# Reordering the front and the end of the first attention in a fused two-attention kernel

## The chip, the cores and the metric

The kernel runs on one core of one Trainium2 chip, as one program. The time is device microseconds; the median of three runs before the change is 1600.74 us, the lowest 1598.55 and the highest 1603.12. A profile is one execution recorded by the hardware profiler; its span runs from the first to the last instruction.

## The reference, cut to what matters

The program computes four residual blocks on 1024 tokens of width 512, all in float32. Only the first block and the entry of the second are touched by the change.

```python
x = x + attn_a(layernorm(x), wq, bq, wk, bk, wv, bv, wo, bo)   # 32 query heads of 16, 8 key groups, softmax over 1024 keys
x = x + ffn(layernorm(x))                                      # dense layer plus top-2 of 8 low-rank experts
x = x + attn_b(layernorm(x), ...)                              # 32 query heads of 128, 8 key groups, causal, 4-bit weights
x = x + ffn(layernorm(x))
```

The first attention's output keeps an unusual order: `out` is swapped to (head, dimension, token) and then reshaped to rows of 512, before `wo`.

## The kernel before, in words

**Engines and order.** TensorE's instructions run in the order in which the code writes them (`tc.manual_schedule` with TensorE alone, L505). The order on VectorE (DVE), ScalarE (ACT), GpSimd (POOL) and the DMA queues of SyncE (SP) and POOL is chosen by the builder's scheduler, which may draw an instruction ahead of others written before it; every queue then runs in its order. So the norm that is written after the pair loop (L549 to L557) has its statistics and rows on DVE and ACT inside the loop in the trace of before, at 407 to 424 us, while its transposes on TensorE stand after the loop.

**Tiling of the first attention** (`attention_a`, L202). 32 heads in 16 pairs of two heads. For a pair, `qs` holds both heads' queries and `ks` the group's keys, each stacked as high and low parts in 64 partitions, and this twice: partitions 0 to 63 (`low`) and 64 to 127 (`high`) hold the same, so that two matmuls on different halves of the array can run beside each other. The stacks are filled by SBUF-to-SBUF DMAs of 64 KB (16 partitions of 4 KB): `stack_keys` (L291) issues 8 for a group of two pairs, `stack_queries` (L297) 16 for a pair. There are three buffers of each (`NS = 3`), so three pairs' queries are stacked in the front.

**Scores for the maximum.** `half_score(i, rows)` (L332) is one matmul of 128 queries against 512 keys into one of three PSUM buffers `sc` (L339) and a maximum over it on DVE (L348). 32 of these make a pair; after the last, three small DVE operations leave the pair's maxima in `largest`. `place_largest` (L358) transposes them on TensorE (L362), copies them on ACT (L364) and sends two DMAs on SP into `ms_q` (L366), from where a second matmul subtracts them in `exponentials` (L375): a score matmul of the transposed kind (L380), the maxima's matmul (L388), and the exponential on ACT (L392). `weighted` (L406) multiplies the exponentials by the values.

**The front.** `keys`, `queries` (L288, through `split`, L269) are projections of four chunks of the contraction; a chunk is two matmul instructions. Between the chunks of `queries(1, 1)` to `queries(3, 1)` the function `lead` (L500) issues scores, so that scores run ahead of the loop: 20 calls of two scores, 40 in all; after the score with number 34 it calls `place_largest` for the first pair.

**The pair loop** (L517 on). For each pair and each of eight blocks of keys (`kt`) one step: `side_by_side` alternates a `low` chain (four scores and one exponential) with a `high` chain (three exponentials); then `place_largest` where maxima are due, and `weighted` of the step before. At `kt` 3 the `tail` (L427) of the pair before is normalised and transposed back into `o_sbs`. At `kt` 5 and 7 of pairs 4, 8 and 12 `project_out(a, h)` (L447) multiplies four pairs' output by `wo` (eight matmul instructions, L453) and adds the product to `x_sb` (L460). At `kt` 7 the stacks three pairs on are refilled, and at pair 12 the expert weights of the second block are loaded into `shared`, whose room the queries of pairs 8 to 15 had.

**The end of the stage.** After the loop: the norm of token blocks 0 to 2 (`stats` L154, `scale` L159 to L161 with a square root on ACT, `rows` L167 and L175, `turned` L190 with eight transposes a block), the last pair's `tail`, and `project_out(3, 0)` and `(3, 1)` between the blocks' transposes. Then the expert part begins with `hidden` (L579), and the norm of block 3.

Of the kernel before, what the change touches and what calls it, by code (L numbers as in the profile page):

```python
# [11 lines left out]
F32 = mybir.dt.float32  # L12
# [29 lines left out]
def kernel(  # L42
# [77 lines left out]
    def place_ffn_weights(room):  # L120
        at = 0
        for name, n, width in ("base", NC_, C), ("ar", NC_, AR), ("b", 1, C), ("bias", 1, C):
            fw[name] = room[:, at : at + n * width].rearrange("p (c o) -> p c o", o=width)
            at += n * width
        return room[:, :at]

    def load_ffn_weights():
        nc.sync.dma_start(fw["ar"][:, :, : E * R], w_a.rearrange("(c p) o -> p c o", p=P))
        nc.sync.dma_start(fw["ar"][:, :, E * R :], w_router.rearrange("(c p) o -> p c o", p=P))
        nc.sync.dma_start(fw["base"], w_base.rearrange("(c p) o -> p c o", p=P))  # L130
        nc.sync.dma_start(fw["b"][:, 0, :], w_b)
        nc.gpsimd.dma_start(fw["bias"][:, 0, :], b_base.partition_broadcast(P))
# [69 lines left out]
    def attention_a():  # L202
# [6 lines left out]
        with ExitStack() as ph:  # L209
# [78 lines left out]
            def queries(c, half, *between):  # L288
                split(q_hls[c], ts(half, C), lambda k: wq_n[:, c, k], bq_sb[:, c : c + 1], *between)

            def stack_keys(g, *engs):  # L291
                for r in range(8):
                    engs[r % len(engs)].dma_start(
                        ks[g % NS][ts(r, DA)].bitcast(F32), k_hl[ts(g, DA), r % 4 // 2].bitcast(F32)
                    )

            def stack_queries(pair, *engs):  # L297

                q, g = qs[pair % NS], pair // 2
                for h in range(2):  # L300
                    row = 2 * (2 * (pair % 2) + h) + g % 2
                    for r in range(8):
                        engs[r % len(engs)].dma_start(
                            q[ts(r, DA), h].bitcast(F32),
                            q_hls[g // 2][ts(row, DA), r % 2].bitcast(F32),
                        )
# [51 lines left out]
            def place_largest():  # L358
                for pair in list(large):
                    both = large.pop(pair)  # L360
                    mp = st_ps.tile([P, C], F32, tag="st", name="mp")
                    nc.tensor.transpose(mp[:, :P], both.bitcast(F32), ident)  # L362
                    mT = work.tile([32, P], F32R, tag="mT", name="mT")
                    nc.scalar.copy(mT, mp[:32, :P])  # L364
                    for r in (0, 64):
                        nc.sync.dma_start(  # L366
                            ms_q[pair % 2][r : r + 2]
                            .bitcast(F32)
                            .rearrange("h j (t q) -> h (j t) q", q=P),
                            mT.bitcast(F32),  # L370
                        )
# [3 lines left out]
            def exponentials(pair, kt, u, rows):  # L375

                if u == 0:
                    pTs[pair, kt] = work.tile([P, 4, C], F32, tag="pT", name="pT", bufs=3)
                st = st_ps.tile([P, C], F32, tag="st", name="st")
                nc.tensor.matmul(  # L380
                    st,
                    ks[pair // 2 % NS][rows, ts(kt, P)],
                    qs[pair % NS][rows, u // 2, ts(u % 2, C)],
                    start=True,
                    stop=False,
                )
                yield
                nc.tensor.matmul(  # L388
                    st, ones[rows], ms_q[pair % 2][rows, u // 2, ts(u % 2, C)], start=False, stop=True
                )  # L390
                yield
                nc.scalar.activation(pTs[pair, kt][:, u], st, AF.Exp, scale=DA**-0.5)  # L392

            def chain(*parts):
                for part in parts:
                    yield from part

            def side_by_side(*two):

                two = list(two)  # L400
                while two:
                    for one in list(two):
                        if next(one, two) is two:
                            two.remove(one)
# [39 lines left out]
                        ALU.mult,  # L444
                    )

            def project_out(a, h):  # L447

                py = st_ps.tile([P, C], F32, tag="st", name="py")
                for c in range(NC_):
                    nc.tensor.matmul(  # L453
                        py,
                        o_sbs[a][:, 4 * h + c, :],
                        wo_n[:, c, :],
                        start=(c == 0),
                        stop=(c == NC_ - 1),
                    )
                nc.vector.tensor_tensor(x_sb[:, a, h, :], x_sb[:, a, h, :], py, ALU.add)  # L460

            def keys(half):
# [5 lines left out]
            stack_queries(0, nc.sync, nc.gpsimd)  # L468
            keys(1)
            stack_keys(0, nc.sync)  # L470
            stack_keys(1, nc.gpsimd)
            stack_queries(1, nc.sync)
            stack_queries(2, nc.sync)

            bo_b = wk_n.rearrange("p k o -> p (k o)").rearrange("p (i o) -> p i o", i=1)
# [11 lines left out]
            def next_score(rows):  # L487
                nonlocal n_score
                n_score += 1
                if n_score <= 32 * PAIRS:  # L490
                    yield from half_score(n_score - 1, rows)

            def scores(n):
                for _ in range(n // 2):
                    side_by_side(next_score(low), next_score(high))


            ahead = iter((2,) * 20)

            def lead():  # L500
                scores(next(ahead))
                if n_score == 34:
                    place_largest()

            with tc.manual_schedule(engines={mybir.EngineType.PE}):  # L505
                for t in range(NT):
                    values(t)
                queries(1, 0)
                queries(1, 1, lead)
                for c in (2, 3):  # L510
                    for half in range(2):
                        queries(c, half, lead)

                wo_n = wq_n.rearrange("p c k o -> p c (k o)")
                nc.sync.dma_start(wo_n, wo.rearrange("(c p) o -> p c o", p=P))
                behind = None
                for pair in range(PAIRS):  # L517
                    for kt in range(NT):
                        side_by_side(
                            chain(  # L520
                                next_score(low),
                                next_score(low),
                                next_score(low),
                                exponentials(pair, kt, 2, low),
                                next_score(low),
                            ),
                            chain(*[exponentials(pair, kt, u, high) for u in (0, 1, 3)]),
                        )
                        if kt % 2 == 0:
                            place_largest()  # L530
                        if behind is not None:
                            weighted(*behind)
                        behind = pair, kt
                        if kt == 3:
                            for item in tails:
                                tail(*item)
                            tails.clear()
                        if kt in (5, 7) and pair % 4 == 0 and pair:
                            project_out(pair // 4 - 1, (kt - 5) // 2)
                        if kt == 7 and pair + NS < PAIRS:  # L540
                            if (pair + NS) % 2 == 0:
                                stack_keys((pair + NS) // 2, nc.sync)
                            stack_queries(pair + NS, nc.sync)
                            if pair + NS == PAIRS - 1:
                                place_ffn_weights(shared)
                                load_ffn_weights()
                weighted(*behind)

                for a in range(3):  # L549
                    norm.stats(a)  # L550
                norm.scale(0, 3)
                for item in tails:
                    tail(*item)
                for a in range(3):
                    xn = wq_in[:, 2 * (a % 2) : 2 * (a % 2) + 2]
                    norm.rows(a, xn)
                    norm.turned(a, xn, bank, False, to_xT)  # L557
                    if a:
                        project_out(3, a - 1)


    class Experts:
# [607 lines left out]
```

## Time and profile before

| what | us |
|---|---|
| median of three runs | 1600.74 |
| the profiled execution | 1601.31 |
| its span | 1599.5 |
| PE busy (matmul row) | 1531.5 (96%) |
| DVE busy | 1241.1 (78%) |
| ACT busy | 783.0 (49%) |
| POOL busy | 482.6 (30%) |
| first projection (keys) starts | 16.7 |
| first score starts | 45.96 |
| pair loop runs | about 84 to 488 |
| hidden layer of the experts starts | 499.6 |

The mean granted clock of TensorE is 0.987 of full speed. Read the busy share of PE with care: matmuls are pipelined and their ends are modelled, so a busy PE is not a PE at its peak; the granted clock stands beside it in the rows by stretch. An idle stretch in the timeline is written behind the instruction that ends it, as "[idle before <-what released it]". The idle time of an engine that is not the bound costs nothing, so waits are looked up at the place of the change and not in the sums over the program.

### The profile page before, as it was taken

The numbers are of one execution on the slowest core, as the hardware profiler recorded it, in microseconds if no ns is written. First come the engines' busy times: TensorE is split into PE (matmuls) and PEld (weight loads), VectorE is DVE, ScalarE is ACT, GpSimd is POOL, SyncE is SP. The second block draws the span as 40 slices with busy tenths as digits, with TensorE's granted clock in tenths as the row PEclk, the third lists the DMA queues.
The fourth block names the chain that finished last, engine by engine and source line by source line (L and its number), as shares of the span: only waits on it lengthen the run. The fifth ranks groups of instructions, "written<-read, shape, count | busy, mean of one in ns | idle before, by whom it ended". The sixth has DMA issues, their size and how long they took to land.

```text
span 1599.5 us, 24080 instructions
## 1 busy us (share of the span) xinstructions
PE 1531.5 (96%) x8119; PEld 990.9 (62%) x8119; DVE 1241.1 (78%) x2290; ACT 783.0 (49%) x1694; POOL 482.6 (30%) x382
## 2 busy tenths in 40 slices
PE   7899999999999989999999999999999999999978
PEld 4244444444445457777777777777777777777764
DVE  4689888799755686788888878888788788788763
ACT  2067666576673245544544544444444444454420
POOL 5200000000103154436336336335435335333120
PEclk9899999999999989999999999999999999999999
DMA  5432322324304133333334334333333334333311
GB/s 126 81 81 47 54 49 48 66 36 88 91 3 110 66 105 125 108 139 124 116 131 139 112 119 135 116 119 126 120 120 121 109 120 129 105 112 129 140 50 53
DMA packets 98010, 158.63 MB, mean 99 GB/s; under 512 B 14320, under 2 KB 53936, under 8 KB 97504
## 3 DMA queue, kind: packets, MB, share of 16 engines
q1 hardware_dynamic: 97024, 155.46, 32.6%
q0 software_dynamic: 864, 1.64, 0.7%
q8 instruction: 65, 1.06, 0.3%
q14 instruction: 57, 0.47, 0.1%
HBM read 33.03 MB, written 6.05 MB: 24 GB/s over the span
## 4 chain that ended last, share of the span: by engine, by line
PE 80%; DVE 12%; ACT 3%; issue 2%; DMA 2%; SPq 1%; POOL 0%; ACTq 0%; DVEq 0%; POOLq 0%
PE pc L888 16%; PE sc L846 15%; PE po L413 7%; PE sc L339 6%; PE pp L782 5%; DVE m L348 5%; PE pp L783 5%; PE tp L878 5%; PE py L782 3%; PE py L783 3%; PE bank L591 3%; PE pp L273 2%; PE st L380 2%; PE py L453 2%; PE st L388 2%
## 5 line engine op out<-in xcount | busy, mean ns | idle before, releaser
L348 DVE TENSOR_REDUCE m<-sc 128x1 f32<-128x512 f32 x512 | 320.7, 681 | 37.3 <-PE st L380 21.7
L855 ACT ACTIVATE x_sb<-sc,m 128x768 f32<-128x768 f32 (+7 forms) x256 | 189.7, 741 | 317.1 <-DVE m L851 311.2
L392 ACT ACTIVATE pT<-st 128x512 f32<-128x512 f32 x512 | 264.7, 603 | 125.6 <-PE st L388 111.7
L846 PE MATMUL sc<-kT,qT 128*128 128x512 f32 (+3 forms) x768 | 293.1, 491 | 4.5 <-ACT x_sb L855 2.9
L851 DVE TENSOR_REDUCE m<-sc 128x1 f32<-128x768 f32 (+7 forms) x256 | 192.7, 753 | 132.5 <-PE sc L849 130.9
L888 PE MATMUL pc<-xT,v_sb 128*128 128x256 f32 (+1 forms) x1024 | 248.5, 373 | 5.0 <-DVE acc L796 2.5
L339 PE MATMUL sc<-ks,qs 64*128 64x512 f32 x512 | 187.0, 455 | 9.8 <-DMA ks<-k_hl 4.5
L857 DVE TENSOR_SCALAR x_sb<-x_sb,total 128x768 f32<-128x768 f32 (+7 forms) x256 | 190.0, 743 | 4.6 <-DVE total L856 0.3
L888 PEld LDWEIGHTS pc<-xT,v_sb 128*128 128x128 f32 x1024 | 176.0, 190 | 21.8 <-DVE acc L796 3.2
L846 PEld LDWEIGHTS sc<-kT,qT 128*128 128x128 f32 x768 | 139.6, 193 | 74.8 <-issue 63.8
L339 PEld LDWEIGHTS sc<-ks,qs 64*128 64x128 f32 x512 | 83.5, 186 | 158.5 <-DVE m L348 128.1
L380 PE MATMUL st<-qs,ks 64*128 64x512 f32 x512 | 177.4, 425 | 2.9 <-ACT pT L392 1.7
L388 PE MATMUL st<-ms_q,ones 64*128 64x512 f32 x512 | 179.0, 414 | 0.3 <-DMA ms_q<-mT 0.3
L923 DVE SCALAR_TENSOR_TENSOR shared<-py,o_sc,shared 128x512 f32<-128x512 f32 x248 | 176.1, 739 | 3.8 <-PE py L783 3.7
L808 POOL TENSOR_TENSOR qT<-acc,cos_sb 128x512 f32<-128x512 f32 x62 | 81.7, 1318 | 298.6 <-DVE total L856 203.1
L782 PE MATMUL pp<-x_hl,w 128*128 128x512 f32 x384 | 167.4, 436 | 1.9 <-DVE acc L796 1.3
L879 ACT COPY xT<-tp 128x512 f32<-128x512 f32 (+2 forms) x320 | 137.2, 471 | 63.9 <-PE tp L878 63.6
L783 PE MATMUL pp<-x_hl,w 128*128 128x512 f32 x384 | 152.7, 398 | 2.4 <-DVE x_hl L740 2.4
L690 POOL TENSOR_SCALAR w<-r 128x512 fp32r<-128x512 int32 x80 | 123.5, 1544 | 102.9 <-PE pp L783 69.8
L796 DVE SCALAR_TENSOR_TENSOR acc<-pp,q_sc,acc 128x512 f32<-128x512 f32 x192 | 142.9, 745 | 13.4 <-ACT acc L794 7.0
L878 PEld LDWEIGHTS tp<-ident_r,moved 128*128 128x128 f32 x1152 | 125.3, 141 | 37.0 <-issue 2.2
L413 PE MATMUL po<-pT,v_sb 128*32 128x512 f32 x1024 | 137.5, 608 | 0.0
(169 smaller groups left out, 2176.4 us busy)
## 6 DMA issues: line engine op xcount, KB each, us to landing
turned<-acc SPq DMA_DIRECT2D x160, 128.0 KB
moved<-x_sb SPq DMA_DIRECT2D x32, 512.0 KB
moved<-x_sb SPq DMA_DIRECT2D x32, 448.0 KB
moved<-x_sb SPq DMA_DIRECT2D x32, 384.0 KB
moved<-x_sb SPq DMA_DIRECT2D x32, 320.0 KB
qs<-shared SPq DMA_DIRECT2D x128, 64.0 KB
r<-in_qwq_dram SPq DMA_DIRECT2D x32, 256.0 KB
r<-in_qwo_dram SPq DMA_DIRECT2D x32, 256.0 KB
```

The costliest lines, as they stand in the source:

```text
L339: nc.tensor.matmul(sc, qs[pair % NS][rows, jj, ts(t, P)], ks[pair // 2 % NS][rows, ts(half, C)], start=True, stop=True,)
L348: nc.vector.tensor_reduce(ms[pair][:, at : at + 1], sc, AX.X, ALU.max, negate=True)
L380: nc.tensor.matmul(st, ks[pair // 2 % NS][rows, ts(kt, P)], qs[pair % NS][rows, u // 2, ts(u % 2, C)], start=True, stop=False,)
L388: nc.tensor.matmul(st, ones[rows], ms_q[pair % 2][rows, u // 2, ts(u % 2, C)], start=False, stop=True)
L392: nc.scalar.activation(pTs[pair, kt][:, u], st, AF.Exp, scale=DA**-0.5)
L413: nc.tensor.matmul(po[ts(u, 32), :], v_sb[:, kt, pair // 2, :], pT[:, u], start=(kt == 0), stop=(kt == NT - 1),)
L782: nc.tensor.matmul(ps, lhsT, high, start=True, stop=False)
L783: nc.tensor.matmul(ps, lhsT, low, start=False, stop=True)
L846: nc.tensor.matmul(sc[:, k0:k1], qT[:, ts(t, P)], kT[:, k0:k1], start=True, stop=(k1 < keys))
L851: nc.vector.tensor_reduce(m, sc[:, :keys], AX.X, ALU.max, negate=True)
L878: nc.tensor.transpose(tp[:, k - k0, :].bitcast(F32R), p[:, ts(k, P)], ident_r)
L888: nc.tensor.matmul(pc[:, 2 * P * i + lo : 2 * P * (i + 1)], v_sb[:, k, ts(g, DB)], place[pair][:, k, lo:], start=(k == 0), stop=(k == 2 * ...
```

## The change

All of it is in `attention_a`. In the front, all 16 DMAs of the two groups' key stacks are issued on SP, the second group's behind the queries of pair 1; before, the second group's eight were on POOL. `lead` issues three, three and no scores in turn, five times, and two at the end: 32 scores over the 16 chunks of `queries(1, 1)` to `queries(3, 0)`. In `queries(3, 1)` only the second chunk is followed by something: `place_largest` for the first pair and three scores. So 35 scores lead instead of 40, and the pair loop takes a fifth score, at the end of the `high` chain, as long as the lead is short, which it is at five steps.

At the end, `project_out(2, 1)` moves from pair 12 to behind the loop, with the last `tail` between its second and third chunk; `project_out(3, *)` stand ahead of the transposes of the norm; the third block's `xn` has a buffer of its own; and the expert weights are placed and loaded at pair 15, `kt` 1, instead of pair 12, `kt` 7.

```diff
@@ -444,7 +444,7 @@
                         ALU.mult,
                     )
 
-            def project_out(a, h):
+            def project_out(a, h, between=lambda: None):
 
 
 
@@ -457,6 +457,8 @@
                         start=(c == 0),
                         stop=(c == NC_ - 1),
                     )
+                    if c == 1:
+                        between()
                 nc.vector.tensor_tensor(x_sb[:, a, h, :], x_sb[:, a, h, :], py, ALU.add)
 
             def keys(half):
@@ -468,8 +470,8 @@
             stack_queries(0, nc.sync, nc.gpsimd)
             keys(1)
             stack_keys(0, nc.sync)
-            stack_keys(1, nc.gpsimd)
             stack_queries(1, nc.sync)
+            stack_keys(1, nc.sync)
             stack_queries(2, nc.sync)
 
             bo_b = wk_n.rearrange("p k o -> p (k o)").rearrange("p (i o) -> p i o", i=1)
@@ -491,25 +493,36 @@
                     yield from half_score(n_score - 1, rows)
 
             def scores(n):
-                for _ in range(n // 2):
-                    side_by_side(next_score(low), next_score(high))
-
-
-            ahead = iter((2,) * 20)
-
-            def lead():
-                scores(next(ahead))
-                if n_score == 34:
-                    place_largest()
+                end = min(n_score + n, 32 * PAIRS)
+                while n_score < end:
+                    if n_score % 2 == 0 and n_score + 1 < end:
+                        side_by_side(next_score(low), next_score(high))
+                    else:
+                        side_by_side(next_score(high if n_score % 2 else low))
 
             with tc.manual_schedule(engines={mybir.EngineType.PE}):
                 for t in range(NT):
                     values(t)
                 queries(1, 0)
+
+
+                ahead = iter((3, 3, 0) * 5 + (2,))
+
+                def lead():
+                    scores(next(ahead))
+
                 queries(1, 1, lead)
-                for c in (2, 3):
-                    for half in range(2):
-                        queries(c, half, lead)
+                for half in range(2):
+                    queries(2, half, lead)
+                queries(3, 0, lead)
+
+                def first_pair():
+                    if n_score == 32:
+                        place_largest()
+                        scores(3)
+
+                ahead = iter((0, 1, 0, 0))
+                queries(3, 1, lambda: next(ahead) and first_pair())
 
                 wo_n = wq_n.rearrange("p c k o -> p c (k o)")
                 nc.sync.dma_start(wo_n, wo.rearrange("(c p) o -> p c o", p=P))
@@ -524,7 +537,10 @@
                                 exponentials(pair, kt, 2, low),
                                 next_score(low),
                             ),
-                            chain(*[exponentials(pair, kt, u, high) for u in (0, 1, 3)]),
+                            chain(
+                                *[exponentials(pair, kt, u, high) for u in (0, 1, 3)],
+                                *[next_score(high)] * (n_score < 32 * pair + 4 * kt + 40),
+                            ),
                         )
                         if kt % 2 == 0:
                             place_largest()
@@ -535,28 +551,31 @@
                             for item in tails:
                                 tail(*item)
                             tails.clear()
-                        if kt in (5, 7) and pair % 4 == 0 and pair:
+                        if kt in (5, 7) and pair in (4, 8, 12) and (pair, kt) != (12, 7):
                             project_out(pair // 4 - 1, (kt - 5) // 2)
                         if kt == 7 and pair + NS < PAIRS:
                             if (pair + NS) % 2 == 0:
                                 stack_keys((pair + NS) // 2, nc.sync)
                             stack_queries(pair + NS, nc.sync)
-                            if pair + NS == PAIRS - 1:
-                                place_ffn_weights(shared)
-                                load_ffn_weights()
+                        if kt == 1 and pair == PAIRS - 1:
+                            place_ffn_weights(shared)
+                            load_ffn_weights()
                 weighted(*behind)
+                project_out(2, 1, lambda: tail(*tails.pop()))
 
                 for a in range(3):
                     norm.stats(a)
                 norm.scale(0, 3)
-                for item in tails:
-                    tail(*item)
+                project_out(3, 0)
+                project_out(3, 1)
                 for a in range(3):
-                    xn = wq_in[:, 2 * (a % 2) : 2 * (a % 2) + 2]
+                    xn = (
+                        wq_in[:, 2 * a : 2 * a + 2]
+                        if a < 2
+                        else q_hls[0][:, 0].bitcast(F32).rearrange("p (i o) -> p i o", i=2)
+                    )
                     norm.rows(a, xn)
                     norm.turned(a, xn, bank, False, to_xT)
-                    if a:
-                        project_out(3, a - 1)
 
 
     class Experts:
```

## The prediction

> **What bounds the kernel now.** I read the page's chain first, then stretches of the front, then the timeline there, then the same for the end of the first attention.
>
> ```profile
> PE 80%; DVE 12%; ACT 3%; issue 2%; DMA 2%; SPq 1%; POOL 0%; ACTq 0%; DVEq 0%; POOLq 0%
> ```
>
> The chain ends on TensorE almost everywhere, so a microsecond of TensorE idleness inside a stage, or of TensorE work at half clock, is paid in full. In the rows by stretch the columns are: stretch, its length, busy us of PE, PEld, DVE, ACT and POOL with their instructions, granted clock, share of the DMA engines, GB/s.
>
> ```profile
> 28.00:46.00 18.00, 14.09 (x82) 9.95 (x80) 4.42 (x11) 1.37 (x2) 8.69 (x18) 0.98 0.83 132
> 46.00:66.00 20.00, 19.37 (x44) 6.44 (x44) 14.65 (x24) 1.37 (x2) 8.83 (x4) 0.84 0.61 104
> ...
> 42.00:46.00 4.00, 0.09 (x2) 0.07 (x1) 0.70 (x1) 0.00 (x0) 0.43 (x1) 0.93 0.82 200
> 46.00:50.00 4.00, 3.37 (x4) 0.99 (x4) 1.38 (x2) 0.00 (x0) 4.00 (x2) 0.50 0.57 101
> ...
> 74.00:78.00 4.00, 1.91 (x5) 0.61 (x5) 2.26 (x7) 0.25 (x1) 0.00 (x0) 0.77 0.01 4
> 78.00:82.00 4.00, 4.00 (x8) 1.14 (x7) 1.29 (x2) 0.00 (x0) 0.00 (x0) 0.50 0.03 8
> ```
>
> See two holes in TensorE (42 to 46, and 74 to 76) and after each a half-rate clock. The timeline names what they wait for:
>
> ```profile
> 38.35 6.54 SPq L293 DMA_DIRECT2D ks<-k_hl  x8
> 44.94 20.23 SPq L303 DMA_DIRECT2D qs<-q_hl  x32
> 45.96 0.76 PE L339 MATMUL sc<-ks,qs 64*128 64x512 f32 x1 [3.91 <-DMA ks<-k_hl]
> 47.35 0.76 PE L339 MATMUL sc<-ks,qs 64*128 64x512 f32 x1 [0.63 <-DMA ks<-k_hl]
> 59.16 1.29 DVE L348 TENSOR_REDUCE m<-sc 128x1 f32<-128x512 f32 x2 [0.28 <-PE sc L339]
> 76.40 0.45 PE L362 MATMUL mp<-ident,largest 128*128 128x128 f32 x1 [2.09 <-DVE largest L353]
> ```
>
> First hole: the stack of the first keys. Second: the pair's maxima, which VectorE has not finished. Between them a lead (2 scores) and a chunk of projection recur every 1.48 us, or 6.1 us per four with the projection's own VectorE step (54.02 to 60.12); VectorE is busy 8 x 0.62 + 0.74 = 5.7 of these.
>
> At the end of the stage:
>
> ```profile
> 410.42 3.70 PE L453 MATMUL py<-wq_n,o_sb 128*128 128x512 f32 x8
> 417.21 1.28 ACT L392 ACT_TABLE_LOAD   x1
> 419.16 0.50 PE L380 MATMUL st<-qs,ks 64*128 64x512 f32 x1 [1.73 <-ACT pT L392]
> 415.90:421.60 5.70, 3.97 (x25) 1.43 (x23) 5.63 (x14) 4.68 (x9) 0.59 (x1) 0.94 0.59 137
> ...
> 488.61 0.66 PE L433 MATMUL pt<-ident,oT 128*128 128x128 f32 x4 [0.78 <-DVE oT L422]
> 495.18 3.60 PE L453 MATMUL py<-wq_n,o_sb 128*128 128x512 f32 x8
> 499.60 5.80 PE L579 MATMUL bank<-shared,xT 128*128 128x136 f32 x48 [0.83 <-issue]
> ```
>
> A usual step of the pair loop takes 2.71 us (weighted at 89.53, 92.23, 94.94). The step with `project_out(2, 1)` takes 6.5. The next two take 5.65 and 3.87: the first norm's statistics, square root, table load and rows, written behind the loop, were drawn forward into it, and the exponentials stand behind them on ACT.
>
> **1. Order of the stacks.** Eight DMAs leave POOL (8 x 0.485 us of issue) and stand on SP between the queries of pairs 1 and 2. Nothing of the first keys' stack is moved on SP; what goes is the 0.5 MB that competed with it, for the engines were 0.8 to 0.9 busy from 30 to 46. Before, SP's issues were stretched until 39.65 (the seventh query DMA held it 3.38 us). Free of this, I let the first key DMA issue between 37.2 and 38.4, then one per 0.6 us, plus the 2.9 us from the eighth's issue (44.31) to the score it released: high keys at 44.3 to 45.4 instead of 47.35. Projections run out at 42.05 as before, so a hole of 2.3 to 3.3 us stays. **The rule against the row:** the Trainium skill's page "TensorE: Matmul & The Clock Gate", Part 1, has the clock halved only after an idle window of some 3.4 us; by it this hole might cost no clock and the gain would be about 5. The trace shows 2.09 us idle at 74.30 followed by clock 0.50, and both drops (45.4 and 76.2, from the mean clocks) lie nine times 3.41 us apart: what counts is how empty a window is, and 42.0 to 45.4 stays empty. So I take the half clock as kept and a gain of **2.0** (bounds 1.5 and 5).
>
> What it costs SP: the page "DMA: Bandwidth & Descriptors", "Issuing engines are not separate DMA queues", says that several issuing engines save only sequencer time, usually small beside the transfer; moving eight DMAs would then be free. The rows differ: 132 GB/s with two queues, 104 with SP alone at engine share 0.61, so SP's issue (20.23 / 32 = 0.63 us) is the limit, and the move adds 8 x 0.63 = 5 us of SP. SP would end near 43 + 40 x 0.63 = 68. Behind it stands the DMA of the maxima, not due before 71: hidden, by 3 us. The bo load and POOL's four additions come forward; nobody waits for them.
>
> **2. Threes.** Six scores per three projection chunks, as before, so the work is equal. VectorE needs 6 x 0.62 + 0.74 x 3/4 = 4.27 us per three chunks against 6.1 x 3/4 = 4.58 now. The added wait is the third score's, for the third of three buffers; behind it on PE stands a chunk, covered by VectorE's backlog in the empty third slot. Leads 4 to 16 are 13 chunks: 13/3 x 0.31 = **1.3** (0.5 to 2).
>
> **3. Last projection and maxima.** Before, from the sixteenth lead (72.34) to the loop's first score (84.0) were 11.6 us: four chunks, eight scores, the 2.09 us wait, half clock to 83. After: two chunks (1.7 us) follow the sixteenth lead, the maxima are ready some 2.9 us after it (two reductions, the projection's step, three of 0.2), so a wait of 1.0; transpose 0.3, three scores 0.5, two chunks 1.7: 5.6 us. The first exponential then needs the maxima's DMA: 0.86 us from transpose to issue, 2.95 from issue to landing (462.19 to 465.14, where TensorE last waited for it), 3.8 in all against 3.0 of cover: 0.8 more. Gain 11.6 - 6.4 = **5.2** (2.5 if this wait empties a clock window).
>
> **4. Five steps of five scores.** VectorE has 4 x 0.62 = 2.48 of 2.71 us; five make 3.1, and the fifth buffer wait stays below that. 5 x 0.4 = **2.0 lost** (1 to 3).
>
> **5. `project_out(2, 1)` out of the loop.** 3.65 us leave pair 12. With the residual missing, the norm can't be drawn forward: 5.65 + 3.87 - 2 x 2.71 = 4.1 leave the next steps, with two table loads. Gain **7.75** (7 to 7.75).
>
> **6. The new end.** Before, 487.8 to 499.6: 11.8 us. After, from 487.8: two chunks of (2, 1) 1.7 (they cover the 0.78 wait for `oT`), tail 0.6, two chunks 1.7, `project_out(3, *)` 6.9, 24 transposes 2.6: 13.6, then the evacuation of the last bank 0.8: 14.4, **2.6 lost** (2 to 4). The norm chain starts when (2, 1) ends at +4.1: addition 0.7, statistics 0.9, root 0.3, two small steps 0.5, rows 0.8, with gaps +8; the transposes want it at +11. The cover is `project_out(3, *)`; without it some 4 us would stand open. The third `xn` frees a wait that was hidden anyway.
>
> **7. Expert weights' loads.** SP and POOL issue them later: base 395.59, the rest at 418 to 420, first read at 499.6. Even issued near 467 they have 30 us. SP has one pair of maxima to move there (462.19). Zero.
>
> Sum: -2.0 - 1.3 - 5.2 + 2.0 - 7.75 + 2.6 = -11.65. The profiled execution took 1601.3 (span 1599.5 and 1.8 around it), so 1589.7; the median shown is 0.6 lower: **1589.1**, chance 0.50.
>
> **Rivals.**
> - Half clock at the maxima (0.20): the waits of step 3 fall in one window. For it: 2.09 us sufficed. Against: the forecast's 1.0 and 0.8 lie 3 us apart. +2.7: 1591.8.
> - No half clock after the first hole (0.13): keys in time, or windows lie differently. -3: 1586.
> - Something drawn forward elsewhere (0.10): engines other than TensorE are ordered by the builder, and the norm's later place may block ACT or VectorE in the expert part, as it did at 416; half of the 7.75 is given back, and two further microseconds: 1595 to 1598, at worst 1606.
> - **Slower: SP becomes the bound (0.07).** The maxima's DMA waits behind 40 stacking DMAs. At 0.71 us each it is late; at about 0.99 the whole gain is gone; at the 1.29 of 27.92 to 38.23 (8 in 10.31 us) the loop starts 22 us late: 1611. Against: 0.63 over 32 in a row with POOL's queue empty.
>
> **Range.** Best ends of all terms: 5 + 2 + 6 - 1 + 7.75 - 2 = 17.75, 1583; worst: 1.5 + 0.5 + 2.5 - 3 + 7 - 4 = 4.5, 1596; the fourth case stretches it to 1598. Within 0.3% (4.8 us, what a measurement here can't tell from none) means above 1595.9. Faster: 0.50 + 0.20 + 0.13 + 0.02 = 0.85; same: 0.06 of the fourth and 0.02 of SP's case, 0.08; slower 0.07.
>
> **What would show it.** First high score near 45 and not 47.35; one half-clock stretch before the loop, not two; the loop's first score near 75; five steps near 3.1 us; no long step after pair 12; hidden layer beginning 14.4 us after the last weighted sum. Wrong if the maxima's DMA issues after 75, if a table load splits the pair loop, or if the transposes at the end wait for VectorE.

## The result, and the profile after

The median is 1592.69 us over eleven runs (1589.33 to 1599.53), against 1600.06 us over eleven of the kernel before (1595.37 to 1605.39). The ratio is 0.9958, with a 95% interval of 0.994 to 0.9976: a gain of 6.7 us, at least 3.8 and at most 9.6. It is about 60% of the 11.65 that the sum promised. The profiled execution took 1591.28 us, span 1589.2, mean granted clock 0.992.

The chain that ended last, by engine, has hardly changed:

```profile
PE 81%; DVE 12%; ACT 3%; issue 2%; DMA 1%; SPq 1%; ACTq 0%; DVEq 0%
```

The front by stretch, with the columns that the prediction names:

```profile
42.00:46.00 4.00, 1.14 (x3) 0.18 (x1) 1.44 (x2) 0.54 (x1) 4.00 (x3) 1.00 0.91 110
46.00:50.00 4.00, 3.00 (x6) 1.09 (x7) 1.29 (x2) 0.00 (x0) 3.72 (x2) 0.61 0.64 108
50.00:54.00 4.00, 4.00 (x7) 1.40 (x7) 1.89 (x3) 0.00 (x0) 0.00 (x0) 0.53 0.66 106
...
74.00:78.00 4.00, 3.29 (x11) 1.47 (x10) 2.96 (x7) 0.58 (x2) 0.00 (x0) 1.00 0.00 0
78.00:82.00 4.00, 3.75 (x16) 1.46 (x14) 3.31 (x7) 2.40 (x3) 0.00 (x0) 1.00 0.27 78
```

The hole at 42 to 46 and the half clock behind it are still there. The second pair, the hole at the maxima and half clock to 83, is gone: the clock is 1.00 from 74 to 82. The timeline says which wait is where:

```profile
32.00 0.75 DVE L276 SCALAR_TENSOR_TENSOR k_hl<-pp,bk_sb,k_hl 128x512 fp32r<-128x512 f32 x1 [2.68 <-ACT k_hl L275]
38.42 5.41 SPq L293 DMA_DIRECT2D ks<-k_hl  x8
44.23 0.47 PE L339 MATMUL sc<-ks,qs 64*128 64x512 f32 x1 [1.55 <-DMA ks<-k_hl]
47.00 0.80 PE L339 MATMUL sc<-ks,qs 64*128 64x512 f32 x2 [2.30 <-DMA ks<-k_hl]
...
59.00 0.73 PE L339 MATMUL sc<-ks,qs 64*128 64x512 f32 x3
59.66 1.12 PE L273 MATMUL pp<-xT,wq_n 128*128 128x512 f32 x2
60.72 1.25 PE L339 MATMUL sc<-ks,qs 64*128 64x512 f32 x3
61.90 1.98 PE L273 MATMUL pp<-xT,wq_n 128*128 128x512 f32 x4
64.34 3.68 DVE L348 TENSOR_REDUCE m<-sc 128x1 f32<-128x512 f32 x6 [0.47 <-PE sc L339]
...
76.66 0.30 PE L362 MATMUL mp<-ident,largest 128*128 128x128 f32 x1 [0.71 <-DVE largest L353]
77.36 1.43 SPq L366 DMA_DIRECT2D ms_q<-mT  x2
80.42 0.50 PE L388 MATMUL st<-ms_q,ones 64*128 64x512 f32 x1 [0.23 <-DMA ms_q<-mT]
...
406.86 1.07 PE L413 MATMUL po<-pT,v_sb 128*32 128x512 f32 x8
408.87 0.49 PE L388 MATMUL st<-ms_q,ones 64*128 64x512 f32 x1 [0.28 <-DMA ms_q<-mT]
410.22 1.06 PE L413 MATMUL po<-pT,v_sb 128*32 128x512 f32 x8
...
475.77 2.40 PE L413 MATMUL po<-pT,v_sb 128*32 128x512 f32 x16
477.09 1.28 ACT L159 ACT_TABLE_LOAD   x1
478.10 1.98 PE L453 MATMUL py<-wq_n,o_sb 128*128 128x512 f32 x4
480.36 8.75 PE L453 MATMUL py<-wq_n,o_sb 128*128 128x512 f32 x20
488.95 1.91 PE L190 MATMUL tp<-ident,wq_in 128*128 128x128 f32 x16
492.58 1.63 PE L598 MATMUL bank<-shared,xT 128*128 128x136 f32 x12 [0.83 <-ACT rstd L159]
```

Read it from the top: TensorE waits 1.55 and 2.30 us for the first keys' DMAs (before: 3.91 and 0.63), so the total wait is shorter. The first score on the high half comes only 0.35 us earlier in the trace's own time, and 1.0 us earlier by the common mark used below. The wait for the maxima fell from 2.09 to 0.71. The step from which `project_out(2, 1)` is gone takes 3.36 us (406.86 to 410.22) in place of 6.51; it isn't quite a usual one of 2.71, since TensorE now waits in it for the DMA of the next pair's maxima (at 408.87): that matmul starts 1.02 us after the score ahead of it (407.85), where 0.34 is usual. Before, the projection lay in this place and covered the DMA. The table load for the norm's square root stands after the last exponential, at 477. The projections run as one block to 488.95, and the transposes follow without a wait.

Since two executions start a little differently (ACT starts to copy the first key projection out of PSUM at 20.34 us before and at 20.97 after), the account below counts from that mark.

| stretch | before | after | difference | forecast |
|---|---|---|---|---|
| mark to fourth lead | 33.68 | 33.22 | -0.46 | -2.0 (step 1) |
| fourth to sixteenth lead | 18.32 | 19.34 | +1.02 | -1.3 (step 2) |
| sixteenth lead to the loop's first exponential matmul | 11.48 | 5.94 | -5.54 | -5.2 (step 3) |
| from there to the fifth weighted sum | 16.53 | 18.55 | +2.02 | +2.0 (step 4) |
| fifth to last weighted sum | 385.08 | 377.75 | -7.33 | -7.75 (step 5) |
| last weighted sum to the hidden layer | 14.17 | 16.81 | +2.64 | +2.6 (step 6) |
| mark to the hidden layer | 479.26 | 471.61 | -7.65 | -11.65 |

Four of the six terms came out within 0.5 us; steps 1 and 2 fell short by 1.5 and 2.3. The experiments look for why, and the last but one of them shows how much of the account is luck.

### The profile page after: what moved, and what is told of

It reads as the page before. It is cut to its first block, busy times and chain, and to the rows that moved or that the text cites. A ratio compares the mean times of both kernels' runs of the same rounds, so it can differ in the third digit from the quotient of the medians.

```text
span 1589.2 us, 24067 instructions
## 1 busy us (share of the span) xinstructions
PE 1523.6 (96%) x8119; PEld 987.8 (62%) x8119; DVE 1240.7 (78%) x2290; ACT 781.4 (49%) x1692; POOL 480.0 (30%) x374
## 3 DMA queue, kind: packets, MB, share of 16 engines
q8 instruction: 65, 1.06, 0.3%
## 4 chain that ended last, share of the span: by engine, by line
PE 81%; DVE 12%; ACT 3%; issue 2%; DMA 1%; SPq 1%; ACTq 0%; DVEq 0%
PE pc L907 16%; PE sc L865 15%; PE po L413 7%; PE sc L339 6%; PE pp L801 5%; DVE m L348 5%; PE pp L802 5%; PE tp L897 5%; PE py L801 4%; PE py L802 3%; PE bank L610 3%; PE st L380 2%; PE py L453 2%; PE st L388 2%; PE pp L273 2%
```

## The experiments

The diffs are against the kernel after the change; medians stand beside those of the kernel before on the same chip. Marks are counted from the first key evacuation, as above.

**The change in two halves.** `front_only` keeps the new front and has the end of before; `end_only` the other way round.

```diff
-   if kt in (5, 7) and pair in (4, 8, 12) and (pair, kt) != (12, 7):
+   if kt in (5, 7) and pair % 4 == 0 and pair:
...
-   project_out(2, 1, lambda: tail(*tails.pop()))
```

In `end_only` also `lead`, the four scores of a step and the place of the maxima are those of before:

```diff
+   stack_keys(1, nc.gpsimd)
    stack_queries(1, nc.sync)
-   stack_keys(1, nc.sync)
...
-   ahead = iter((3, 3, 0) * 5 + (2,))
+   ahead = iter((2,) * 20)
```

> The kernel before with the front's edits alone (stack order, threes, five steps of five scores); the end as before. If the parts add up, the fifth weighted sum of the pair loop stands near 98.0 us (100.35 before) and the hidden layer starts 2.4 us before the old 499.6, so 497.2; time about 2 to 3 us below the kernel before. Rival, the front gives nothing by itself: fifth weighted sum within 0.5 us of 100.35.

> The kernel before with the end's edits alone (third projection's second half behind the loop, last projection ahead of the transposes, third buffer, later loads). If the parts add up: the front as before (fifth weighted sum at 100.35), no long steps after pair 12, last weighted sum near 478.4 (485.43 before, 7.05 less), hidden layer near 495.2; time 4 to 5 us below before. Rival, the parts lean on each other: a table load still splits the pair loop and the last weighted sum stays above 482.

Measured: `front_only` 1595.42 us against 1600.00, ratio 0.9973 (0.9964 to 0.9983); `end_only` 1593.34, ratio 0.9964 (0.995 to 0.9977). To the hidden layer the front alone gains 2.7 us (476.54 against 479.26) and the end alone 5.5 (473.72); together 8.3, against 7.65 for both in one. But 1.0 of the 5.5 stands ahead of the fifth weighted sum (79.03 us after the mark against 80.01), where `end_only` is the kernel before: its half clock at the maxima lasted 3.4 us in place of 6.8. Without it the halves make 7.3 by these profiles. The medians show more, 4.3 and 5.8 us beside 6.7 for both, with intervals of 1.5 to 2.9 us on each side that don't exclude a plain sum. Either way the shortfall belongs to the front, which was forecast at 6.5.

**The keys' stack against its competitor.** Step 1 said that the second keys' stack on POOL slowed the first keys. `keys_on_pool` puts it back there; `q0_sp` takes the other POOL transfers away, half of the first queries.

```diff
    stack_keys(0, nc.sync)
+   stack_keys(1, nc.gpsimd)
    stack_queries(1, nc.sync)
-   stack_keys(1, nc.sync)
```

```diff
-   stack_queries(0, nc.sync, nc.gpsimd)
+   stack_queries(0, nc.sync)
```

> The changed kernel with the second group's eight key DMAs back on POOL. Counted from the end of the first key projection's ACT step (20.97 in the changed kernel), the first high score stands at 26.0 in the changed kernel and 27.0 in the kernel before. If moving the second stack is worth only that 1 us, this run has 27.0, the same stretch of half clock, and the loop starts less than 1.5 us later than in the changed kernel. By the prediction the second stack is what stretches SP's issue, worth 2 us or more.

> The changed kernel with all sixteen DMAs of the first queries' stack on SP, none on POOL. If POOL's eight DMAs are what fills the engines (share 0.93 at 100 GB/s, against 0.61 at 104 with SP alone), SP issues at 0.6 us without stretch: sixteen in 9.7 us, the first key DMA again about 38.4, engine share from 32 to 42 near 0.6 and a shorter time from the last key's issue to the first high score (2.9 or less, 3.8 in the changed kernel). Rival, the engines are full of the bytes themselves: sixteen take 12 us or more and the first high score comes 3 us later.

`keys_on_pool`, one run of 1589.39 us: the loop starts 58.48 us after the mark, against 58.50 in the kernel after. From its timeline:

```profile
37.69 6.83 SPq L293 DMA_DIRECT2D ks<-k_hl  x8
46.18 1.56 PE L339 MATMUL sc<-ks,qs 64*128 64x512 f32 x3 [4.33 <-DMA ks<-k_hl]
```

The issue is stretched again (6.83 us for eight, as the 6.54 of before), and it costs nothing at the loop. The first high score comes 26.8 us after the mark, 0.8 later than in the kernel after; but the half clock, too, ends 0.9 us sooner after the mark (31.9 against 32.8). So the move that step 1 priced at 2 us is worth less than one for the keys and nothing at the loop, by one execution of each. `q0_sp`, one run of 1594.69 us, its timeline:

```profile
28.81 11.32 SPq L303 DMA_DIRECT2D qs<-q_hl  x16
40.23 5.05 SPq L293 DMA_DIRECT2D ks<-k_hl  x8
47.42 0.80 PE L339 MATMUL sc<-ks,qs 64*128 64x512 f32 x2 [2.03 <-DMA ks<-k_hl]
```

and its stretch from 40 to 42, where the kernel after has a DMA share of 0.95 at 98 GB/s:

```profile
40.00:42.00 2.00, 2.00 (x6) 0.85 (x5) 0.00 (x0) 0.00 (x0) 2.00 (x2) 1.00 0.62 100
```

The DMA engines are a third emptier. From the end of the keys' issue (45.28) to the released score take 2.1 us instead of 3.2 (43.83 to 47.00). But sixteen queries now stand ahead on SP, so the keys' issue ends later, and the high keys come 26.19 us after the mark against 26.03. Competition costs the keys about a microsecond, by one execution of each; their place behind the queries on SP takes that back.

**The keys ahead of the queries.** `keys_first` projects and stacks the first keys before the first queries.

```diff
-   keys(0)
+   for half in range(2):
+       keys(half)
+   stack_keys(0, nc.sync)
    for half in range(2):
        queries(0, half)
    stack_queries(0, nc.sync, nc.gpsimd)
-   keys(1)
-   stack_keys(0, nc.sync)
    stack_queries(1, nc.sync)
```

> The changed kernel with both halves of the key projection ahead of the first query projection, and the first keys' stack issued ahead of the queries' stack. If the first high score is late because the keys' transfers stand behind the sixteen of the queries, which fill the engines from 30 to 38 us, both stacks are there by about 41 to 43, the hole before the first scores closes, the half clock at 46.7 to 53.5 goes, and the loop starts 4 to 6 us earlier (first score near 74 to 75). Rival, the sum of the bytes is the limit (1.5 MB at 100 GB/s from 28.5): first high score still above 45 and the loop less than 2 us earlier.

Measured: 1584.95 us against 1600.00, ratio 0.9906 (0.9892 to 0.9921), clear of the interval of the kernel after. Timeline, then stretches:

```profile
25.80 5.07 SPq L293 DMA_DIRECT2D ks<-k_hl  x8
32.67 17.01 SPq L303 DMA_DIRECT2D qs<-q_hl  x24
43.28 0.49 PE L339 MATMUL sc<-ks,qs 64*128 64x512 f32 x1
43.99 0.51 PE L339 MATMUL sc<-ks,qs 64*128 64x512 f32 x2 [0.22 <-issue]
```

```profile
40.00:44.00 4.00, 3.78 (x11) 1.36 (x9) 0.74 (x2) 0.69 (x1) 2.32 (x5) 1.00 0.99 174
44.00:48.00 4.00, 4.00 (x11) 1.52 (x11) 3.69 (x7) 0.00 (x0) 0.00 (x0) 1.00 0.83 131
```

The first score follows the projection without a wait, though the DMA engines are 0.99 busy; there is no hole, so no half clock, and the loop starts 51.83 us after the mark, 6.7 earlier. That is what the hole that step 1 meant to shorten cost, with the half clock behind it, and it was to be had by the order of the front. The run moves the keys' projection and their place in SP's list together and doesn't part the two. But in the kernel after, the keys were complete at 32.75 us (the end of VectorE's step) and their first DMA issued at 38.42: 5.7 us went to the queries ahead of them on SP.

**Twos and threes.**

```diff
-   ahead = iter((3, 3, 0) * 5 + (2,))
+   ahead = iter((2,) * 16)
```

> The changed kernel with two scores after each of the sixteen chunks instead of three, three, none. If TensorE is the limit in the threes (4.81 us per three chunks, against 4.58 in the kernel before), the loop starts about 1 us earlier than in the changed kernel (its first score 79.5, so 78.5). By the prediction (VectorE the limit, threes fill it) it starts 1.3 us later, at 80.8.

Measured: 1590.75 us, ratio 0.9942 (0.9929 to 0.9955). The loop starts 58.94 us after the mark, 0.44 later than with threes, so both expectations missed. The stretches say why it can't be read there:

```profile
50.00:54.00 4.00, 4.00 (x8) 1.28 (x6) 2.42 (x4) 0.00 (x0) 0.00 (x0) 0.50 0.65 104
54.00:58.00 4.00, 4.00 (x9) 1.27 (x8) 2.56 (x5) 0.69 (x1) 0.00 (x0) 0.69 0.62 106
```

In this execution the half clock lasted until 56.5 instead of 53.7, and hid what the twos bring. From 57.01 to 73.66, at full clock, eleven chunks with their twos took 1.51 us each; threes take 1.61 (4.81 us for three). To be rid of the hole, the next run combines both.

> Keys projected and stacked first, and two scores after each chunk. In the run of twos a half clock that lasted one window longer hid the comparison. With no half clock in the front, TensorE has 1.61 us a chunk in the threes and 1.51 in the twos: the loop starts 1.0 to 1.5 us earlier than with the keys first and threes (first score 73.5, so 72 to 72.5). Rival, the twos empty a clock window again: half clock before the loop, and the loop not earlier.

`keys_first_twos` (the edits of `keys_first` and `twos` together): 1582.64 us (1581.99 to 1585.03) against 1599.60, ratio 0.9906 (0.989 to 0.9923). The loop starts 50.92 us after the mark, 0.91 earlier than in `keys_first`, just short of the 1.0 expected. The ratios of the two kernels are equal, so the whole run doesn't tell them apart; the timeline does. Here `keys_first_twos`:

```profile
45.51 1.13 PE L273 MATMUL pp<-xT,wq_n 128*128 128x512 f32 x2
46.56 0.50 PE L339 MATMUL sc<-ks,qs 64*128 64x512 f32 x2
47.00 1.13 PE L273 MATMUL pp<-xT,wq_n 128*128 128x512 f32 x2
```

Two scores and a chunk take 1.49 us, all of it TensorE at work, and three of these 4.47 (4.54 on average with the slower ones, in `twos`). In the threes of the kernel after, the first three scores take 0.66, the second three 1.18 (60.72 to 61.90), and the chunks 1.06 and 1.91: 4.81. The second trio takes 0.52 us more than the first because its third score has no free buffer of the three. VectorE, meanwhile, waits 0.47 us in every three chunks.

**`project_out(2, 1)` back in the loop.**

```diff
-   if kt in (5, 7) and pair in (4, 8, 12) and (pair, kt) != (12, 7):
+   if kt in (5, 7) and pair % 4 == 0 and pair:
...
-   project_out(2, 1, lambda: tail(*tails.pop()))
+   tail(*tails.pop())
```

> The changed kernel with the third projection's second half back in pair 12; the rest of the end as changed. If the long steps come from this half and from the norm that it lets forward, the steps after pair 12 are long again (about 6.5, 5.6, 3.9), the square root's table load stands in the pair loop, the last weighted sum comes 7 us later than 475.8, and the end is 3.4 us shorter (hidden layer 13.4 after the last weighted sum's start instead of 16.8): hidden layer at 496.2, time 3 to 4 us above the changed kernel. Rival, the expert weights' transfers at 415 to 424 made those steps long: then only 3.6 us come back.

Measured: 1598.05 us against 1599.60, ratio 0.9999 (0.9985 to 1.0013): without this part the change brings nothing that can be measured. Its timeline:

```profile
406.20 3.70 PE L453 MATMUL py<-wq_n,o_sb 128*128 128x512 f32 x8
406.41 1.28 ACT L159 ACT_TABLE_LOAD   x1
...
484.60 0.66 PE L433 MATMUL pt<-ident,oT 128*128 128x128 f32 x4 [0.79 <-DVE oT L422]
485.88 7.13 PE L453 MATMUL py<-wq_n,o_sb 128*128 128x512 f32 x16 [0.63 <-DVE o_sb L438]
```

The table load is back in the middle of the loop, and from the fifth to the last weighted sum it takes 384.84 us against 377.75: 7.1 lost. At the end only 1.5 come back (15.35 against 16.81 to the hidden layer), not 3.65, since the wait for `oT` (0.79) and one for `o_sb` (0.63), which the projection covered, stand open. Net 5.6; the ratios differ by 0.0041, which is 6.6 us.

**The same kernels again.** Unchanged, to see what differs between executions.

> The changed kernel once more, unaltered, for a second profiled execution. If the half-clock stretches in the first head of the second attention (552 to 559 alone in the first profile, three of them in the profile before) depend on where the clock's windows fall and not on the program, their number or place differs here, while the marks of the first attention, counted from the first key projection's ACT step, stay within 0.5 us: fifth weighted sum at 77.05, last one at 454.8, hidden layer at 471.6.

> The kernel before once more, unaltered. Marks from the first key projection's ACT step within 0.5 us of the first profile: fifth weighted sum at 80.0, last one at 465.1, hidden layer at 479.3. In the run with the end's edits alone the same front stood 1 us earlier (79.0) with a half clock of one window instead of two ahead of the loop; if that is a matter of the windows, this run shows one value or the other.

`after_again` took 1592.92 us and reached the hidden layer 471.86 us after the mark (471.61 in the first profile); `before_again` took 1601.58 and 477.08 (479.26). In `before_again` the half clock at the maxima lasted 3.4 us (76 to 80) instead of 6.8, and the loop started 1.6 us earlier:

```profile
78.00:82.00 4.00, 4.00 (x11) 1.45 (x10) 2.55 (x4) 0.21 (x1) 0.00 (x0) 0.80 0.03 8
```

The first profile has a clock of 0.50 there, and `end_only`, with the same front, is like `before_again`. From the sixteenth lead to the loop's first exponential matmul these two take 10.1 us in place of 11.48. So between a quarter and a third of the 7.65 in the account is the luck of the first profile, most of it in step 3.

After the stage the luck goes on. The stretches, before and then after, of work behind the hidden layer that the change doesn't touch (after is there some 7 us further on in the program):

```profile
574.00:580.00 6.00, 4.29 (x13) 2.61 (x13) 5.54 (x10) 1.01 (x2) 2.76 (x2) 0.82 0.39 125
...
586.00:592.00 6.00, 4.07 (x11) 2.02 (x10) 4.11 (x7) 1.47 (x3) 3.28 (x3) 0.72 0.58 206
```

```profile
574.00:580.00 6.00, 4.34 (x22) 3.03 (x20) 5.93 (x10) 2.54 (x8) 5.23 (x4) 1.00 0.19 44
...
586.00:592.00 6.00, 5.54 (x34) 3.94 (x32) 4.48 (x7) 3.23 (x9) 4.22 (x4) 1.00 0.43 133
```

From the hidden layer to the end the kernel before takes 1099.9 us and the kernel after 1096.6. That is why the two profiled executions lie 10.0 us apart at their ends, and 7.0 at the hidden layer (499.60 and 492.58); the medians differ by 7.4. In `after_again` a half-clock stretch of 6.8 us does fall at 568 to 576.

**A shorter lead.** In the best version, the lead of 38 scores in place of 40, so that fewer steps take a fifth score.

```diff
-   *[next_score(high)] * (n_score < 32 * pair + 4 * kt + 40),
+   *[next_score(high)] * (n_score < 32 * pair + 4 * kt + 38),
```

> Keys first, twos, and a lead of 38 scores in the loop instead of 40: three steps of five scores instead of five. Each step of five takes 3.3 us against 2.71, so two fewer give 1.2 us at the loop's sixth step if nothing else is late; two scores more fall into later steps, at most 0.1 us. Rival: the maxima of the next pair come half a step later (in the step of kt 6, not 5) and TensorE waits for them at each pair, up to 0.3 us in fifteen pairs: 4 us lost.

Measured: 1621.43 us, ratio 1.0126 (1.0102 to 1.0149), 39 us slower than `keys_first_twos`: a bad miss. The rival named the right wait, at 0.3 us a pair. The view of the tile `mp` lists the idle time of TensorE ahead of the 16 transposes of the maxima, in us and times; first with lead 38, then with 40:

```profile
  DVE largest L353: 20.9, 13
  DVE mv L155: 6.7, 3
```

```profile
  DVE largest L353: 0.7, 1
```

And the first such place by stretch, with lead 38:

```profile
90.00:94.00 4.00, 2.25 (x17) 1.16 (x21) 2.96 (x8) 2.37 (x6) 0.00 (x0) 1.00 0.01 2
94.00:98.00 4.00, 4.00 (x24) 1.99 (x20) 2.05 (x4) 1.37 (x3) 0.00 (x0) 0.57 0.05 12
```

`place_largest` is called at even `kt`. With 40, a pair's thirty-second score is the last of an odd step (`4 * 5 + 40 + 4 = 64`), and a whole step of 2.7 us covers the reduction and the three small operations of VectorE. With 38 it falls into the even step itself, and TensorE stands 1.75 us before most transposes (all 16 waits sum to 27.6 us; three of 2.2 us are put down to a step of the norm on VectorE, `mv`). The step concerned grows from 3.28 to 4.76 us, which is some 22 us in 15 pairs. Eleven of the waits are followed by a stretch of 3.4 us at half clock, at most 1.7 each or 19 in all. From the fifth to the last weighted sum the run loses 38.0 us, so these two make it up. Lead 40 isn't the length of a buffer but a phase against the parity of `kt`.

## Why the prediction was right, and where its numbers were off

The gain lies where four of the six terms put it. The forecast of 1589.1 us was 3.6 below the median because the first two steps, which were to gain 3.3 us, together lost 0.6.

**Step 1 failed in its size.** The prediction put -2.0 on the ground that "what goes is the 0.5 MB that competed with it"; the stretch brought -0.46 with both keys moved, and with the competitor restored in `keys_on_pool` the high keys came 0.8 us later and the loop began at the same time. The mis-sized parts are three: the first key DMA issued at 38.42, the late end of "between 37.2 and 38.4"; one each 0.68 us, not 0.6; and 3.2 us from the end of the issue to the released score, where before had 2.5 (from the eighth key's issue at 44.31 to the score at 47.35 are 3.0 and not the sum's 2.9). The prediction itself noted that nothing of the first keys is moved on SP, and didn't draw the conclusion: the keys stood ready for 5.7 us behind the eight queries on SP, whose issue took 9.74 us. `keys_first`, which puts keys ahead of queries, has no hole. That the half clock after the hole would stay was right, against the rule of an idle window of some 3.4 us that the prediction weighed: the stretch from 46 to 54 has 0.61 and 0.53 after two idle spells of 1.55 and 2.30. The same rows exclude the rival that expected no half clock here.

**Step 2 failed in its sign.** It took VectorE as the limit (4.27 us per three chunks, against 4.58 before), and the period came to 4.81. Neither engine alone sets that: TensorE's own work is 4.29 (two trios of 0.66, chunks of 1.06 and 1.91), and VectorE idles too. The 0.86 us for a chunk holds only where chunks stand in a row; a chunk with scores on half the array on either side takes 1.06, in twos and threes alike. And the third buffer's wait, which was to be "covered by VectorE's backlog", stands open in every second trio for 0.5 us, because VectorE is 0.47 us idle just before the first trio and then has six reductions to do. (Between leads 4 and 16 lie 12 chunks, and not the 13 of the sum, which changes little.) The prediction compared the average demand of two engines and not the order in which they hand over.

**Step 3 was right in its parts, and its size is partly luck.** The row has -5.5 against -5.2, and the parts fit: 0.71 us of wait for the maxima (forecast 1.0), 0.23 for their DMA (0.8), no half clock. The rival that saw half clock here (1591.8 us, beside the median of 1592.69) hit the time by another way; the clock of 1.00 from 74 to 82 excludes it. But the 11.6 us it started from hold a half clock of 6.8 us, and against `before_again` or `end_only`, with 3.4, the stretch gains 4.1 to 4.2.

**Step 4 was right in sum.** Each of three steps of five scores costs 0.6 us more than a usual one (3.30 against 2.71; 3.1 forecast); the first two steps cost less. **Step 5** came to -7.05 in the three steps concerned (3.36, 2.90 and 2.72 us in place of 6.51, 5.65 and 3.87), and `project_back` gives it by itself. Its parts were other than forecast, though the sum was near. Steps aren't all of 2.71: behind the second projection of pair 8, where no norm is drawn in, the kernel before has 6.50, 3.65 and 2.70, and pair 11, without a projection, has 2.71, 2.99 and 2.71. So the projection cost 4.4 us in its two steps and not 3.65, the norm 3.2 and not 4.1. Part of the norm's share is half clock, which the prediction did not count by itself; before has, behind its wait of 1.73 us at 419.16,

```profile
421.00:424.00 3.00, 3.00 (x13) 0.70 (x12) 1.23 (x3) 2.91 (x6) 0.28 (x1) 0.50 0.36 113
```

and the records of the granted clock show a stretch of 3.4 us there in before, `before_again`, `front_only` and `project_back`, and none where the projection stands behind the loop. The missing 0.7 is the longer first step (3.36 against 2.71) with its wait for the maxima's DMA at 408.87, which the projection had covered; `end_only` has the same wait. Why that DMA comes late here and at few other pairs isn't followed up. "The norm can't be drawn forward" holds for its root, table load and rows; statistics of blocks that were complete still are (0.68 us of VectorE at 405.11), but TensorE isn't seen to wait for them. **Step 6**, +2.6, was exact, and `project_back` shows its two hidden waits. **Step 7** is zero: the loads issue from 392.6 to 417.3 us although they are written into pair 15, because the scheduler draws them there from either place, and nothing is seen to wait for them. No run puts this part alone back.

**The rivals.** SP as the bound didn't come: the stacks end at 69.3 us (68 forecast), 4.1 later than before, and SP is idle until the maxima's DMA at 77.36. That this is after 75, which the prediction took for a sign of SP being late, is the lateness of steps 1 and 2: the transpose itself stands at 76.66. The first high score near 45 and the loop near 75 missed in the same way. As to work drawn forward elsewhere, the rows of the account leave no room for it up to the hidden layer: behind the fifth weighted sum they are within 0.5 us of the forecast.

**The total.** The sum missed by 4.0 us at the hidden layer (1.5 and 2.3 in steps 1 and 2). The medians' gain, 6.7 to 7.4, is close to what the account has left, and that is partly chance: against `before_again` the two executions of the kernel after gain 5.2 and 5.5 at the hidden layer.

## What to carry to other kernels

A transfer that is late has a place in a queue before it has a competitor: read what its issuing engine did ahead of it, and whether its input was ready, before pricing bandwidth; here the competitor was worth less than a microsecond, and putting the keys ahead of the queries, in projection and queue, 6.7 us. Where two engines alternate through a few buffers, follow one period of the handover by hand, since both can be idle in it although their mean load fits. Before an effect of idleness is priced from one profile, look how long the half clock behind it lasts in a second execution. And a projection moved out of a pipelined loop may be worth twice its own duration, if the work that depends on it was drawn into the loop by the scheduler (7.05 us for 3.65 here).

## What the runs showed of the hardware beyond the forecast

The granted clock falls by windows of about 3.4 us: stretches at half clock lasted 3.4, 6.8 or 10.2 us. How long they are behind a hole of 2 to 4 us varies between executions of one kernel (3.4 or 6.8 us at the maxima of before). Behind the first hole it was 6.8 us in the kernel after and 10.2 in `twos`, which is the same program up to the hole. Eleven runs of the kernel after spread over 10.2 us, with mean clocks from 0.988 in the slowest to 0.991 and 0.992 in the fastest; one of 1595.03 us has 0.992, so the clock isn't all of it; the four of `keys_first`, whose front has no hole, over 1.4 us. That the holes make the spread is suggested by this and not shown, since four runs are few and the later half-clock stretches are in all kernels.
